# A two-layer row kernel on one core: row sums over sixteen rows, one ring of buffers for x and layer 0's outputs, later accumulating loads, and a PSUM ring turned by one tile

## The chip, the cores and the metric

The kernel runs on one core of a Trainium2 chip. The metric is the device time of one execution in microseconds. The engines are named as the profile names them: PE is TensorE (PEld its weight loads), DVE is VectorE, ACT is ScalarE, POOL is GpSimd, and SP is SyncE, which here only issues DMAs. A letter q after an engine (SPq) is its queue.

## What is computed

The input x has 384 x 384 positions of 128 channels, all in float32. Two layers follow one another. Layer 0 is a triangle update: a layer norm, two gated projections, a product over k for each channel, a second layer norm, an output projection and a gate, with x added. Layer 1 is a gated row mix: each row's output is scaled by the sum of `right` over that whole row, and a layer norm ends it.

```python
# layer 0
z = _layernorm(x, norm_g, norm_b)
left = (z @ Wl + bl) * jax.nn.sigmoid(z @ Wlg + blg)
right = (z @ Wr + br) * jax.nn.sigmoid(z @ Wrg + brg)
core = jnp.einsum('bikh,bjkh->bijh', left, right)
zo = _layernorm(core, onorm_g, onorm_b) @ Wout + bout
g = jax.nn.sigmoid(x @ Wg + bg)
x = x + g * zo
# layer 1, pair = x
left = pair @ W_left + b_left
right = pair @ W_right + b_right
gate = jax.nn.sigmoid(pair @ W_gate + b_gate)
left = left + (pair @ W_eq + b_eq)
right_sum = jnp.sum(right, axis=2, keepdims=True)
out = left * right_sum
out = out * gate
out = out @ W_out + b_out
return _layer_norm(out + pair, ln_scale, ln_bias)
```

## The kernel before

The program runs in three stages, one after the other, and every instruction is kept in the order in which the code writes it, on its engine's queue. What sets the order is therefore the code itself; what sets the time is which wait ends last.

**Stage 1 (to 1131 us)** goes over x in 144 chunks of eight rows by 128 positions. It makes row statistics (DVE), shifts x by them (POOL, L268), transposes (PE, L277), copies the result to SBUF (ACT, L279), and multiplies it with the four joined projection matrices (PE, L313) into a PSUM tile `pr` that holds two rows in two banks. ACT makes the sigmoid (L320) and DVE the gated product `lr` (L322), which empties the tile. `back` (L304) takes one `pr` tile for two rows, 576 in all, from a ring of three (`pps`, six banks); two single banks belong to `tps`. Ahead of the loop, one tile of the same ring, `p1`, serves the matmuls of `busy`, which only keep PE running while the first data arrive, and those of `fold`, which fold the norm's parameters into the weights. The stage stores its products `lr_d`, the shifted and transposed x `xt_d`, and the shifts `nd_d`.

**Stage 2 (1133 to 1876 us)** goes over the 128 hidden channels: 18 PE instructions for each (L477) into a PSUM tile `pc` of three banks, two such tiles in turn. POOL copies the right operand (L452 to L459), ACT and DVE copy the result out and sum it for the second norm.

**Stage 3 (1876 us to the end)** works in turns t, about one for each of the 384 rows. One turn does, for different rows:

- `front(f)`: PE's gate projection `pg` (L598) and ACT's sigmoid `gT`, for row f - 4. The transposed row `xT` comes, for the first 16 rows, from PE transposes (L609) and a copy into a work buffer; for later rows it is loaded as the sum of two DMAs into one tile of the ring `xp`: a plain broadcast load of `nd_d` (`load_x`, L548, SP's queue), and on top of it an accumulating load of `xt_d` (`add_x`, L556, POOL's queue).
- `scale_core(t)`: the core row times the norm's root, `cs` (POOL, L634). Its two operands are loaded by `load_core` (L566, L570) through SP's queue, into rings of three.
- `last` of the rows that were in layer 1 three turns before: DVE L718, which frees their PSUM tile `py`, then POOL L724.
- `right_sums(i0, i1)`: once all rows of a group are known, one small product `pq` of their column sums with W_right (L620), and its bias (DVE, L622), giving `rsum`.
- `layer0(t - 2)`: PE `pr` (L643), then two DVE operations (L644, L646); the second writes `x1T` and adds up its column sums into `tot`.
- `out_matrix`: ACT scales W_out by a row's `rsum` (L654).
- `gated_left(t - 3)`: PE `pg2` and `pl` (L660, L661; the profile calls both gate tiles pg), ACT `g2`, DVE `u` (L665).
- `layer1` and `stats1` for the rows that `at[t]` lists: PE L672 and L673 into `py` (a ring of four banks, `ps2`), DVE statistics (L687, L689), and for each second row POOL's root chain (L691 to L696), of which L692 is the power. `norm1` (ACT, L707) follows two turns later.

All other PSUM tiles of a turn (pg, pq, pr, pg2, pl) come from one ring of four banks, `ps`. At every fourth turn from t = 19 to 91 a list of `pieces` computes the rest of the second norm's root, on ACT, POOL and DVE, beside the turns.

A row can enter `layer1` only when its group's `rsum` is known, at the earliest three turns after the group's last row has come up. The table `turn` (L580 to L588) sets this: rows go one a turn, a group's first row not before `i1 + 3`, and near the end a row now and then shares the turn of the row before it, so that the lag shrinks. Before, groups have eight rows up to row 336, then four, and two in the last eight: 56 groups. The lag of layer 1 is 11 turns up to row 336 and 7 in the end; four turns (347, 354, 361, 368) hold two rows of layer 1 on the way, and 383 and 386 in the tail.

Buffers in SBUF: `fp` holds `xT` and `gT`, 13 each; `lp` holds `x1T` and `u`, 11 each; `wp` four each of `cs`, `g2` and `wo`. In stage 3 the pools lie in the space that stages 1 and 2 have left.

Of the kernel before, what the change touches and what calls it, by code (L numbers as in the profile page):

```python
# [8 lines left out]
F32 = mybir.dt.float32  # L9
# [5 lines left out]
P = 128  # L15
# [4 lines left out]
def triangle_then_gated_row_kernel(ctx: ExitStack, tc: tile.TileContext, a: dict, out: bass.AP):  # L20
# [13 lines left out]
    x = a["x"].rearrange("b i j c -> (b i) j c")  # L34
    y = out.rearrange("b i j c -> (b i) j c")
    N, _, C = x.shape
    H = a["L0_conv_Wl"].shape[1]
# [7 lines left out]
    A = 9  # L45
# [35 lines left out]
    with ExitStack() as ctx2:  # L81
# [17 lines left out]
        with tc.tile_pool(name="p1w", bufs=6, side="right") as wp, \  # L99
# [46 lines left out]
            warm = const([P, 1], "warm")  # L146
            seq(nc.scalar.activation(warm, mhalf[:, 0:1], AF.Sigmoid))
            wz = const([P, 4 * H], "wz")
            p1 = pps.tile([P, 2, 4 * H], F32, tag="pr", name="p1")[:, 0]
            pgb = tps.tile([P, 4, P], F32, tag="pt", name="pgb")[:, 0, 0:2]  # L150
            g0 = const([P, 1], "g0")

            def busy(n):

                for _ in range(n):
                    seq(nc.tensor.matmul(
                        p1, lhsT=avg, rhs=avg.unsqueeze(1).to_broadcast([P, 4, P]), start=True, stop=True
                    ))

            def fold():  # L160
# [357 lines left out]
    with ExitStack() as ctx3:  # L518
        def pool(name, bufs, **kw):
            return ctx3.enter_context(tc.tile_pool(name=name, bufs=bufs, reuse_waits="tile", **kw))  # L520

        xp, fp, inp, op = pool("p3x", 6), pool("p3f", A + 4), pool("p3in", 3), pool("p3out", 3)
        wp, sp = pool("p3w", 4), pool("p3s", 4)
        lp = pool("p3l", 11)
        ps2, ps = pool("p3ps2", 4, space=PSUM), pool("p3ps", 4, space=PSUM)

        def bank(name):
# [1 line left out]

        def work(name, pool=wp):  # L530
            return pool.tile([P, N], F32, tag=name, name=name)

        cols = [slice(b * P, (b + 1) * P) for b in range(NB)]
        lnsb = lns.unsqueeze(1).to_broadcast([P, NB, C])
# [41 lines left out]

        firsts = list(range(0, N - 48, 8)) + list(range(N - 48, N - 8, 4)) + list(range(N - 8, N, 2))
        group, sums, turn = {}, {}, []  # L580
        for i0, i1 in zip(firsts, firsts[1:] + [N]):
            sums[i1 + 2] = i0, i1
            for i in range(i0, i1):
                group[i] = i0, i - i0
                t = turn[-1] + 1 if i else 0
                turn.append(max(i1 + 3, t - (i0 >= N - 48 and i % 8 == 1 and t > i + 7 or i in (N - 7, N - 3))))
        assert turn[N - 8:] == [N - 1, N - 1, N, N + 1, N + 2, N + 2, N + 3, N + 4]
        at = {t: [i for i in range(N) if turn[i] == t] for t in range(N + 5)}  # L588

# [3 lines left out]
        def front(f):  # L593

            r = rows.get(f - L)
            if r:
                pg = bank("pg")
                seq(nc.tensor.matmul(pg[:, :N], lhsT=wg0, rhs=r["xT"], start=True, stop=True))  # L598
                gT = r["gT"] = work("gT", fp)
                seq(nc.scalar.activation(gT, pg[:, :N], AF.Sigmoid, bias=bg0))  # L600
            if f < N:
                i0, n = f // RG * RG, f % RG
                if f >= TR:
                    xT = xts[i0][:, n]
                else:
                    xT = work("xT", fp)
                    pxt = ps2.tile([P, 512], F32, tag="py", name="pxt") if f < A else bank("pxt")
                    for s in cols:
                        seq(nc.tensor.transpose(pxt[:, s], xin[i0][:, n, s], ident))  # L609
                    if 4 <= f < A:  # L610
                        seq(nc.vector.tensor_copy(xT, pxt[:, :N]))
                    else:
                        seq(nc.scalar.copy(xT, pxt[:, :N]))
                rows[f] = {"xT": xT}

        def right_sums(i0, i1):

            q = quad[i0]
            pq = bank("pq")
            seq(nc.tensor.matmul(pq[:, :i1 - i0], lhsT=wright, rhs=q["tot"][:, :i1 - i0], start=True, stop=True))  # L620
            q["rsum"] = sp.tile([P, 8], F32, tag="rsum", name="rsum")
            seq(nc.vector.tensor_scalar(q["rsum"][:, :i1 - i0], pq[:, :i1 - i0], bright, None, ALU.add))  # L622

        def scale_core(i):
# [11 lines left out]
        def layer0(i):  # L636

            r = rows[i]
            m, n = group[i]
            if n == 0:  # L640
                quad[m] = {"tot": sp.tile([P, 8], F32, tag="tot", name="tot")}
            pr = bank("pr")
            seq(nc.tensor.matmul(pr[:, :N], lhsT=wc, rhs=r["cs"], start=True, stop=True))  # L643
            seq(nc.vector.scalar_tensor_tensor(pr[:, :N], pr[:, :N], bz, r["gT"], ALU.add, ALU.mult))  # L644
            x1T = r["x1T"] = work("x1T", lp)
            seq(nc.vector.scalar_tensor_tensor(  # L646
                x1T, pr[:, :N], bout1, r["xT"], ALU.add, ALU.add, accum_out=quad[m]["tot"][:, n:n + 1]
            ))
# [7 lines left out]
        def gated_left(i):  # L656

            r = rows[i]
            pg2, pl = bank("pg2"), bank("pl")
            seq(nc.tensor.matmul(pg2[:, :N], lhsT=wgate, rhs=r["x1T"], start=True, stop=True))  # L660
            seq(nc.tensor.matmul(pl[:, :N], lhsT=wleft, rhs=r["x1T"], start=True, stop=True))  # L661
            g2 = work("g2")
            seq(nc.scalar.activation(g2, pg2[:, :N], AF.Sigmoid, bias=bgate))  # L663
            u = r["u"] = work("u", lp)
            seq(nc.vector.scalar_tensor_tensor(u, pl[:, :N], bleft, g2, ALU.add, ALU.mult))  # L665

        def layer1(i, py):
# [80 lines left out]
        for t in range(N + 3):  # L748

            while f < min(N + L, t + max(L, A - t // 3)):  # L750
                front(f)
                f += 1
            if t % RG == 0:
                load_core(t + 2 * RG)
            if t >= 2 and fetched <= f + 16:
                load_x(fetched)
                fetched += RG
            if t >= 7 and (t % 4 == 1 or t < 12) and added <= f + 8:
                add_x(added)
                added += RG  # L760
            if t < N:
                scale_core(t)
            if t >= 16 and t % 4 == 3 and pieces:
                step, b, s = pieces.pop(0)
                step(b, s)
                if step is root:
                    step, b, s = pieces.pop(0)
                    step(b, s)
                if step is newton and s == cols[-1]:
                    store_rstd(b)  # L770
            done = at.get(t - 3, [])
            for i in done:
                last(i)
            if t in sums:
                right_sums(*sums[t])
            if 2 <= t < N + 2:
                layer0(t - 2)
            for i in at[t + 1]:
                out_matrix(i)
            if t >= 3:  # L780
                gated_left(t - 3)
            for i in at[t]:
                layer1(i, ps2.tile([P, 512], F32, tag="py", name="py"))
                stats1(i)
            for i in at.get(t - 2, []):
                norm1(i)
            store()
# [53 lines left out]
```

## Time and profile before

| | |
|---|---|
| median of 3 runs | 3296.77 us (3295.2 to 3296.97) |
| the profiled execution | 3295.14 us, span 3293.4 us |
| granted clock, mean | 0.998 |
| L313 PE MATMUL, stage 1 | 1040.1 us busy, x2304 |
| L477 PE MATMUL, stage 2 | 743.3 us busy, x2304 |
| L620 PE MATMUL (pq) | 15.9 us busy, x112 |
| L692 POOL (root chain) | 257.9 us busy, x192, mean 1343 ns |
| L556 POOL DMA issue | 85.8 us busy, x92, mean 932 ns; landing 6.7, 9.5, 15.3 us (least, median, most) |
| POOL and DVE from 2400 to 2800 us | 348.70 and 351.02 us busy of 400 |
| DMA engines from 2400 to 2800 us | 0.97 of their time, 273 GB/s |

Busy time is summed over an engine's instructions; a float32 product shows as two matmul records, a transpose as one. The records of consecutive matmuls overlap, so it is their starts that are to be compared. The number behind an arrow is the idle time of the engine ahead of an instruction, and the name is that of the instruction that ended the wait.

### The profile page before, as it was taken

To read this page: it belongs to the slowest core of one execution; us is meant where nothing else is said; L and a number is where in the kernel's file an instruction comes from. 1 tells how busy PE (TensorE), PEld (TensorE's weight loads), DVE (VectorE), ACT (ScalarE), POOL (GpSimd) and SP (SyncE) were. 2 spreads that over 40 slices of the span, in tenths; PEclk is the share of its full clock that TensorE was granted. 3 is DMA by queue.
4 is the path that set the end of the run, shared out by engine and by line. 5 is a ranking of instruction groups with operands and counts; after the bars stand their busy time and mean duration, and the time that the engine had idled before them with its cause. 6 is when DMAs were issued, how large, how long until landed. Compare 5 with 4: busy or idle time off the path is not lost.

```text
span 3293.4 us, 48397 instructions
## 1 busy us (share of the span) xinstructions
PE 3269.7 (99%) x12496; PEld 1991.3 (60%) x12496; DVE 2500.1 (76%) x8040; ACT 1940.3 (59%) x4055; POOL 2287.2 (69%) x3300
## 2 busy tenths in 40 slices
PE   9999999999999999999999999999999999999998
PEld 4544444444444566666666666767777777777776
DVE  7777777777777655555555588888888888888888
ACT  4555555555555433334333467777777777777776
POOL 6555555555555566656566578898888888888887
PEclk9999999999999999999999999999999999999999
DMA  6998998998999499999999999999999999999993
GB/s 164 273 279 259 277 280 258 275 281 260 276 281 263 148 284 279 284 282 285 281 286 282 286 295 265 277 273 274 276 270 274 279 271 268 278 278 269 275 260 109
DMA packets 922056, 873.72 MB, mean 265 GB/s; under 512 B 24834, under 2 KB 836868, under 8 KB 921780
## 3 DMA queue, kind: packets, MB, share of 16 engines
q1 hardware_dynamic: 906532, 796.03, 78.3%
q0 software_dynamic: 13440, 72.56, 12.9%
q8 instruction: 103, 1.69, 0.2%
q10 hardware_dynamic: 1808, 2.03, 0.2%
q14 instruction: 173, 1.42, 0.1%
HBM read 508.63 MB, written 361.89 MB: 264 GB/s over the span
## 4 chain that ended last, share of the span: by engine, by line
PE 94%; POOL 3%; DVE 1%; ACT 1%; DMA 1%; issue 1%; POOLq 0%; DVEq 0%; ACTq 0%
PE pr L313 30%; PE pc L477 23%; PE py L672 7%; PE pr L643 7%; PE pg L598 7%; PE pl L661 7%; PE pg L660 7%; PE pt L277 4%; PE py L673 3%; POOL cs L634 1%; POOL rs L692 1%; POOL yt L724 1%; DMA xt<-nd_d 1%; ACT py L707 0%; DVE st L687 0%
## 5 line engine op out<-in xcount | busy, mean ns | idle before, releaser
L313 PE MATMUL pr<-wz,zt 128*128 128x512 f32 x2304 | 1040.1, 593 | 0.7 <-ACT zt L279 0.7
L320 ACT ACTIVATE sg<-pr,rs 128x256 f32<-128x256 f32 x1152 | 483.8, 471 | 497.9 <-PE pr L313 361.3
L477 PE MATMUL pc<-rr,lrh 128*128 128x384 f32 x2304 | 743.3, 486 | 2.0 <-DVE lr L322 2.0
L322 DVE SCALAR_TENSOR_TENSOR lr<-pr,rs,sg 128x256 f32<-128x256 f32 x1152 | 504.8, 480 | 267.5 <-ACT sg L320 218.8
L313 PEld LDWEIGHTS pr<-wz,zt 128*128 128x128 f32 x2304 | 414.2, 190 | 411.0 <-issue 345.9
L477 PEld LDWEIGHTS pc<-rr,lrh 128*128 128x128 f32 x2304 | 452.0, 196 | 293.6 <-issue 2.8
L707 ACT ACTIVATE py<-py,nm,rs 128x128 f32<-128x128 f32 x1149 | 494.5, 431 | 198.1 <-POOL rs L696 115.0
L672 PEld LDWEIGHTS py<-wo,u 128*128 128x128 f32 x2304 | 377.1, 191 | 100.6 <-DVE yt L718 0.6
L634 POOL TENSOR_TENSOR cs<-ct,rt 128x384 f32<-128x384 f32 x380 | 428.5, 1131 | 4.9 <-DMA rt<-rstd_d 4.9
L488 DVE TENSOR_TENSOR csum<-csum,ct 128x1152 f32<-128x1152 f32 x127 | 176.8, 1392 | 333.9 <-ACT ct L486 333.9
L724 POOL TENSOR_TENSOR yt<-yt,lnb 128x384 f32<-128x384 f32 x380 | 425.6, 1121 | 3.4 <-DVE yt L718 3.2
L486 ACT COPY ct<-pc 128x1152 f32<-128x1152 f32 x127 | 142.2, 1120 | 446.9 <-PE pc L477 446.9
L672 PE MATMUL py<-wo,u 128*128 128x128 f32 x2304 | 402.7, 275 | 0.3 <-ACT wo L654 0.3
L258 POOL TENSOR_SCALAR sd<-mv 128x8 f32<-128x8 f32 (+1 forms) x145 | 28.7, 198 | 427.4 <-DVE mv L245 427.3
L268 POOL TENSOR_TENSOR z<-xt,nd 128x512 f32<-128x512 f32 x288 | 300.4, 1043 | 34.6 <-POOL z L268 29.4
L687 DVE BATCH_NORM_STATS2 st<-py 128x6 f32<-128x128 f32 x1152 | 266.1, 287 | 76.0 <-PE py L673 74.5
L643 PE MATMUL pr<-cs,wc 128*128 128x384 f32 x768 | 315.2, 492 | 1.3 <-POOL cs L634 1.3
L673 PE MATMUL py<-ident,x1T 128*128 128x128 f32 x1152 | 314.0, 273 | 0.0
L661 PE MATMUL pl<-x1T,mat_L_conv_W_left 128*128 128x384 f32 x768 | 311.5, 487 | 1.4 <-ACT gT L600 1.4
L660 PE MATMUL pg<-x1T,mat_L_conv_W_gate 128*128 128x384 f32 x768 | 310.8, 486 | 1.1 <-ACT g L663 0.9
L598 PE MATMUL pg<-xt,mat_L_conv_Wg 128*128 128x384 f32 x736 | 298.4, 487 | 0.0
L458 POOL COPY rr<-lrh 128x768 f32<-128x768 f32 x128 | 176.3, 1378 | 159.5 <-DMA lrh<-lr_d 159.4
(129 smaller groups left out, 4932.5 us busy)
## 6 DMA issues: line engine op xcount, KB each, us to landing
lr_d<-lr SPq DMA_DIRECT2D x128, 1024.0 KB, 7.1
lrh<-lr_d SPq DMA_DIRECT2D x128, 768.0 KB, 7.7
xt_d<-zt SPq DMA_DIRECT2D x288, 256.0 KB, 5.5
xt<-in_x_dram SPq DMA_DIRECT2D x143, 512.0 KB, 6.3
ct<-core_d SPq DMA_DIRECT2D x95, 768.0 KB, 6.1
rt<-rstd_d SPq DMA_DIRECT2D x95, 768.0 KB, 7.6
out_dram<-yt SPq DMA_DIRECT2D x94, 768.0 KB, 8.9
core_d<-ct SPq DMA_DIRECT2D x125, 576.0 KB, 8.8
```

The costliest lines, as they stand in the source:

```text
L313: seq(nc.tensor.matmul(pr[:, r, :], lhsT=zts[n, q][:, 2 * half + r, :], rhs=wz, start=True, stop=True))
L320: seq(nc.scalar.activation(sg[r], pr[:, r, 2 * H:], AF.Sigmoid, scale=rs[r]))
L322: seq(nc.vector.scalar_tensor_tensor(t[:, :, c * XR + r0 + r, :], pr[:, r, :2 * H].rearrange("k (h s) -> k h s", s=2), rs[r], sg[r].rearra ...
L477: seq(nc.tensor.matmul(banks[ib], lhsT=t[:, kb, ib * P:(ib + 1) * P, 0], rhs=rr[:, kb], start=(kb == 0), stop=(kb == NB - 1),))
L598: seq(nc.tensor.matmul(pg[:, :N], lhsT=wg0, rhs=r["xT"], start=True, stop=True))
L634: seq(nc.gpsimd.tensor_tensor(cs, ct[:, i % RG], rt[:, i % RG], ALU.mult))
L643: seq(nc.tensor.matmul(pr[:, :N], lhsT=wc, rhs=r["cs"], start=True, stop=True))
L660: seq(nc.tensor.matmul(pg2[:, :N], lhsT=wgate, rhs=r["x1T"], start=True, stop=True))
L661: seq(nc.tensor.matmul(pl[:, :N], lhsT=wleft, rhs=r["x1T"], start=True, stop=True))
L672: seq(nc.tensor.matmul(py[:, s], lhsT=r["u"][:, s], rhs=r["wo"], start=True, stop=False))
L707: seq(nc.scalar.activation(py[:, s], py[:, s], AF.Identity, bias=bias, scale=scale))
L724: seq(engine.tensor_tensor(yt, yt, lnbb, ALU.add))
```

## The change

It has four parts.

1. Stage 1 takes two tiles from the ring of `pr` ahead of the loop, not one: `p0` for `busy`, `p1` for `fold`. Each later `pr` tile lies one slot further round the ring.
2. In stage 3, `xT` of the first 16 rows and `x1T` share one ring of 20 buffers (tag x in `lp`), `u` gets a pool of its own with 18, and `gT` has 9. The pools are opened in another order, and so lie at other addresses.
3. The groups of the row sums have 8, 8, 8, 12, 12, then sixteen times 16, six times 8, six times 4 and four times 2 rows: 37 groups. `tot` and `rsum` become 16 wide. By the table `turn`, no row enters layer 1 in turns 35 to 38 and 63 to 66, the lag of layer 1 is 19 turns for rows 48 to 305, and twelve turns (every fourth from 324 to 368) hold two rows; 383 and 386 stay as they are.
4. The accumulating loads begin in turn 9 and go out in every fourth turn. Rows 16, 20, 24 and 28 are issued in turns 9, 13, 17 and 21; before, in turns 7, 8, 10 and 17. In the steady part a load is issued 7 turns ahead of its first use and not 11.

```diff
-            p1 = pps.tile([P, 2, 4 * H], F32, tag="pr", name="p1")[:, 0]
+            p0, p1 = (pps.tile([P, 2, 4 * H], F32, tag="pr", name=n)[:, 0] for n in ("p0", "p1"))
...
-                        p1, lhsT=avg, rhs=avg.unsqueeze(1).to_broadcast([P, 4, P]), start=True, stop=True
+                        p0, lhsT=avg, rhs=avg.unsqueeze(1).to_broadcast([P, 4, P]), start=True, stop=True
...
-        xp, fp, inp, op = pool("p3x", 6), pool("p3f", A + 4), pool("p3in", 3), pool("p3out", 3)
-        wp, sp = pool("p3w", 4), pool("p3s", 4)
-        lp = pool("p3l", 11)
+
+        xp, lp, fp, inp = pool("p3x", 6), pool("p3l", 20), pool("p3f", A), pool("p3in", 3)
+        wp, sp, op, up = pool("p3w", 4), pool("p3s", 4), pool("p3out", 3), pool("p3u", 18)
...
+        def work_x(name):
+
+            return lp.tile([P, N], F32, tag="x", name=name)
...
-        firsts = list(range(0, N - 48, 8)) + list(range(N - 48, N - 8, 4)) + list(range(N - 8, N, 2))
+        sizes = [8] * 3 + [12] * 2 + [16] * ((N - 128) // 16) + [8] * 6 + [4] * 6 + [2] * 4
+        assert sum(sizes) == N
         group, sums, turn = {}, {}, []
-        for i0, i1 in zip(firsts, firsts[1:] + [N]):
+        i1 = 0
+        for size in sizes:
+            i0, i1 = i1, i1 + size
             sums[i1 + 2] = i0, i1
             for i in range(i0, i1):
                 group[i] = i0, i - i0
                 t = turn[-1] + 1 if i else 0
-                turn.append(max(i1 + 3, t - (i0 >= N - 48 and i % 8 == 1 and t > i + 7 or i in (N - 7, N - 3))))
+                turn.append(max(i1 + 3, t - (i >= N - 80 and i % 5 == 1 and t > i + 7 or i in (N - 7, N - 3))))
...
-                    xT = work("xT", fp)
+                    xT = work_x("xT")
...
-            q["rsum"] = sp.tile([P, 8], F32, tag="rsum", name="rsum")
+            q["rsum"] = sp.tile([P, 16], F32, tag="rsum", name="rsum")
...
-                quad[m] = {"tot": sp.tile([P, 8], F32, tag="tot", name="tot")}
+                quad[m] = {"tot": sp.tile([P, 16], F32, tag="tot", name="tot")}
...
-            x1T = r["x1T"] = work("x1T", lp)
+            x1T = r["x1T"] = work_x("x1T")
...
-            u = r["u"] = work("u", lp)
+            u = r["u"] = work("u", up)
...
-            if t >= 7 and (t % 4 == 1 or t < 12) and added <= f + 8:
+            if t >= 9 and t % 4 == 1:
                 add_x(added)
                 added += RG
```

## The prediction

> **What bounds the kernel now.** I read three views in this order: the page (busy times, slices, chain), the timeline of single stretches, and the table of waits.
>
> ```profile
> PE 3269.7 (99%) x12496; PEld 1991.3 (60%) x12496; DVE 2500.1 (76%) x8040; ACT 1940.3 (59%) x4055; POOL 2287.2 (69%) x3300
> ...
> POOL 6555555555555566656566578898888888888887
> ...
> PE 94%; POOL 3%; DVE 1%; ACT 1%; DMA 1%; issue 1%; POOLq 0%; DVEq 0%; ACTq 0%
> ```
>
> PE is busy 99% of the span and is 94% of the chain. So the change can gain only by removing PE work or one of PE's few idle stretches, about 24 us in all (3293.4 - 3269.7), much of it at the very start and end. Everything it adds to other engines is free unless PE comes to wait for it. In the last stage (from 1876 us) POOL is the next busiest.
>
> PE's timeline in the last stage prices a group's row sum:
>
> ```profile
> 2513.23 0.81 PE L598 MATMUL pg<-xt,mat_L_conv_Wg 128*128 128x384 f32 x2
> 2513.88 0.81 PE L643 MATMUL pr<-cs,wc 128*128 128x384 f32 x2
> 2514.52 0.81 PE L660 MATMUL pg<-x1T,mat_L_conv_W_gate 128*128 128x384 f32 x2
> ...
> 2516.81 0.81 PE L598 MATMUL pg<-xt,mat_L_conv_Wg 128*128 128x384 f32 x2
> 2517.46 0.28 PE L620 MATMUL pq<-tot,mat_L_conv_W_right 128*128 128x8 f32 x2
> 2517.60 0.89 PE L643 MATMUL pr<-cs,wc 128*128 128x384 f32 x2
> 2518.32 0.81 PE L660 MATMUL pg<-x1T,mat_L_conv_W_gate 128*128 128x384 f32 x2
> ```
>
> A turn repeats every 3.58 us (2513.23 to 2516.81). From pg (L598) to pg2 (L660) it takes 1.29 us without the row sum and 1.51 us with it: **0.22 us a group**. Near the end, at 3250.76 us, a group of two rows gives the same 1.51, so columns hardly enter.
>
> The boundary of stages 1 and 2, PE then DVE:
>
> ```profile
> 1127.41 3.60 PE L313 MATMUL pr<-wz,zt 128*128 128x512 f32 x8
> 1133.05 1.21 PE L477 MATMUL pc<-rr,lrh 128*128 128x384 f32 x3 [2.04 <-DVE lr L322]
> ```
> ```profile
> 1130.21 0.88 DVE L322 SCALAR_TENSOR_TENSOR lr<-pr,rs,sg 128x256 f32<-128x256 f32 x2 [0.95 <-ACT sg L320]
> 1131.92 0.88 DVE L322 SCALAR_TENSOR_TENSOR lr<-pr,rs,sg 128x256 f32<-128x256 f32 x2 [0.84 <-ACT sg L320]
> ```
>
> The first stage-2 matmul starts 0.25 us after DVE has emptied the last pr tile (1132.80). The tile before that was empty at 1131.09.
>
> The start of stage 3, POOL then PE:
>
> ```profile
> 1900.01 0.94 POOL L556 DMA_DIRECT2D xt<-xt_d  x1 [3.91 <-DMA xt<-nd_d]
> 1900.65 1.32 POOL L634 TENSOR_TENSOR cs<-ct,rt 128x384 f32<-128x384 f32 x1
> 1901.78 1.06 POOL L556 DMA_DIRECT2D xt<-xt_d  x1
> 1902.39 2.42 POOL L634 TENSOR_TENSOR cs<-ct,rt 128x384 f32<-128x384 f32 x2
> 1913.33 0.88 POOL L556 DMA_DIRECT2D xt<-xt_d  x1 [8.52 <-DMA xt<-nd_d]
> 1913.94 3.19 POOL L634 TENSOR_TENSOR cs<-ct,rt 128x384 f32<-128x384 f32 x3
> ```
> ```profile
> 1915.29 0.91 PE L643 MATMUL pr<-cs,wc 128*128 128x384 f32 x2 [1.35 <-POOL cs L634]
> ```
>
> The third accumulating load, in turn 10, sits in POOL's queue before that turn's cs and waits 8.52 us for its plain load; PE ends by waiting for that cs.
>
> **What the skill says.** *TensorE: Matmul & The Clock Gate*, Part 2, "Step-by-step", says the next weights are loaded while the current matmul runs. The trace agrees for full tiles (a 0.19 us load under 0.81 us of matmul); eight columns are too short a cover, which fits the flat 0.22 us. The same page, Part 1, "Architectural detail", calls ACT, DVE and GpSimd strict FIFOs: the cs held behind the load above is that. *PSUM — Partial Sum Buffer*, "PSUM bank collisions", says to guard PSUM by bank: the 2.04 us wait is such a guard, on a buffer and not on data. *DMA: Bandwidth & Descriptors*, "SWDGE vs HWDGE", says only GpSimd can issue accumulating DMAs; here each issue holds POOL for 0.93 us.
>
> **The change, part by part.** Figures are against the profiled execution, 3295.14 us (span 3293.4).
>
> *Groups.* 56 groups become 37. Nineteen row sums go, 19 x 0.22 = **-4.2 us** on PE. The 16 remaining wide ones stream eight columns more; at 0.645/384 us a column that is 0.013 us each, 0.2 us in all if none hides, 0 if all does: I take 0. DVE loses 19 x 0.216 us, off the path.
>
> *Bank waits.* With a pq the turn takes five tiles of the ring of four, so pl needs the bank of the same turn's pg, which ACT must read first. The trace shows PE idle there at 2025, 2055, 2113, 2143 and 2201 us (0.17 to 0.35 us); with the restart these turns are 0.53, 0.52, 0.61, 0.44 and 0.62 us longer than other pq turns, 2.7 us together. All lie where the pieces of the root run (turns 19 to 91), which make ACT's norms late. That stretch had row sums in turns 26, 34, 42, ... 90; it now has them in 26, 38, 50, 66 and 82, two of them in light turns. I keep two stalls of 0.45: **-1.8 us**, between 0 and -2.7. The stall at 2032 us (table loads for the root) stays.
>
> *PSUM ring.* The ring has three tiles. One more tile at its head moves the last of the 576 pr tiles off the slot that stage 2 opens in; that slot's last user is now the one before, free at 1131.09, so pc can start at 1131.34, but PE is only done at 1131.01. **-1.7 us**, or 0 if stage 2's three banks touch both slots. Next late would be the copies into rr for the third k-block: they follow the last lr and end at 1133.3, needed 12 matmuls x 0.32 = 3.9 us after the start, 1135.2. POOL's copies for the second channel end at 1135.2, needed at 1137.1. Covered. The busy matmuls only change their target.
>
> *Accumulating loads.* Same 92 issues, now rows 16, 20, 24 in turns 9, 13, 17, not 7, 8, 10. On POOL, cs 7 and 8 move ahead of the first, cs 9 to 12 ahead of the second; core loads waiting in SP's queue for those cs (L566 at 1902.00) go out earlier. The load for row 24, landed at 1913.3, is asked for only around 1934. PE's hole is 1915.29 - 1913.78 = 1.5 us plus 0.1 of restart: **-1.6 us**; 0 if rt for row 12, issued at 1891.78 into saturated DMA, is as late. Later each load is issued 7 turns before its row is used, 25 us (21 through the light turns), not 11; landing takes 6.7 to 15.3 us. Covered.
>
> *Rings and schedule.* xT and x1T share 20 buffers, u gets 18, gT 9. Layer 1 follows its row by up to 19 turns, so x1T's buffer is free 3 turns before it is rewritten and u's 2: 0 us, and cover lost only if layer 1 slipped two turns (7 us). The new addresses keep early tiles out of stage 2's latest buffers; PE's waits there (0.56 us on PSUM, 0.23 on x1T data) aren't about addresses: 0. Turns 35 to 38 and 63 to 66 have no layer 1 (light, four matmul pairs, 2.58 us); in exchange twelve turns, every fourth from 324 to 368, have two (before: four, every seventh). PE's total is the same. But POOL: four turns take it 13.4 us (2500.19 to 2513.57), a fifth row adds yt 0.96 and half a root chain 1.08, so 15.4 us against PE's 4 x 3.58 + 1.00 + 0.22 = 15.5. Before, seven turns with eight rows were 25.5 against 26.3, and PE lost 0.15 us (its row period at 3180 was 4.72, not 4.57). The cost of a double is thus between 0 and POOL's whole extra 2.04 us; I take 0.07 each, **+0.8 us**, since POOL still just fits.
>
> Sum: -4.2 - 1.8 - 1.7 - 1.6 + 0.8 = **-8.5 us**. The profiled execution would be 3286.6; the median of runs, 1.6 us higher before (3296.77), gives 3288.3: I say 3288.
>
> **Rivals.** *B, part of it only:* PE gets just the row sums; ring and start are replaced by a next wait, and the bank stalls move to other turns. 3296.77 - 4.2 = 3292.6. For: the pieces of the root still fall beside row sums, and DMA is at 1.01 of its share from 1890 to 1920. Against: the next releases computed above have 1.9 us or more of slack. *C, slower:* POOL sets the pace in the twelve double turns. If its 2.04 us comes wholly on top each time, 24.5 - 9.3 = +15: 3312. It undoes the gain from 0.8 us a double on. For: 99% load, and py's four banks leave no spare turn after a double. Against: the four doubles before nearly ran free.
>
> **How the numbers follow.** Forecast 0.64, B 0.24, C 0.12. About 0.2% (6.6 us) is what tells from no change: the forecast lies beyond it, B within. C passes it in 0.09 and stays within in 0.03: faster 0.64, same 0.27, slower 0.09. Low end: all gains at their full size, no cost, 10.2, and 2 of scatter: 3284.5. High end: B with some cost in the doubles: 3294.
>
> **What would show it.** Right: 74 pq matmuls (before 112); pc starting within 0.4 us of the last pr; no PE wait on cs around 1914; fewer waits of pl on gT; double turns at 4.57 us. Wrong: double turns of 5 us and more, with py waiting for yt (L718) and L707 for rs; pc still waiting for lr; PE waiting for cs or xt in turns 12 to 16.

## The result, and the profile after

| | before | after |
|---|---|---|
| median of 17 runs each | 3296.17 us (3294.28 to 3298.72) | 3289.34 us (3288.54 to 3290.4) |
| after / before, 95% interval | | 0.998 (0.9972 to 0.9987) |
| the profiled execution | 3295.14 us, span 3293.4 us | 3289.21 us, span 3287.4 us |
| first pg2 (L660, now L667) of row 14, of row 376 | 1933.29, 3248.47 us | 1929.64, 3242.29 us |

The change is worth 6.8 us by the medians, 4.3 to 9.2 us by the interval, and 5.9 us between the two profiled executions (6.0 by their spans). In the whole text that follows "after" is the changed kernel; its line numbers in stage 3 are 4 higher than those of before in the loads and 7 higher from `front` on.

Two lines of the page of after: busy times, and the chain by engine.

```profile
PE 3265.1 (99%) x12458; PEld 1986.6 (60%) x12458; DVE 2481.1 (75%) x8021; ACT 1933.4 (59%) x4055; POOL 2281.7 (69%) x3300
...
PE 91%; POOL 6%; ACT 1%; issue 1%; DMA 1%; DVE 1%; POOLq 0%; ACTq 0%
```

PE lost 4.6 us of work (3269.7 to 3265.1) and still bounds the kernel. But POOL's share of the chain has doubled, from 3% to 6%. That is a first hint of where a part of the gain stayed.

The boundary of stages 1 and 2 in after, PE and then DVE:

```profile
1127.17 3.60 PE L313 MATMUL pr<-wz,zt 128*128 128x512 f32 x8
1131.09 9.28 PE L477 MATMUL pc<-rr,lrh 128*128 128x384 f32 x28 [0.32 <-DVE lr L322]
```
```profile
1129.96 0.88 DVE L322 SCALAR_TENSOR_TENSOR lr<-pr,rs,sg 128x256 f32<-128x256 f32 x2 [0.95 <-ACT sg L320]
1131.68 0.88 DVE L322 SCALAR_TENSOR_TENSOR lr<-pr,rs,sg 128x256 f32<-128x256 f32 x2 [0.84 <-ACT sg L320]
```

Stage 2's first product starts 0.25 us after the last but one `pr` tile is empty (1129.96 + 0.88 = 1130.84) and while DVE still has the last one to empty. PE's idle time there is 0.32 us where it was 2.04.

The start of stage 3 in after, POOL:

```profile
1897.99 0.93 POOL L560 DMA_DIRECT2D xt<-xt_d  x1 [0.75 <-DMA xt<-nd_d]
1899.16 1.00 POOL L641 TENSOR_TENSOR cs<-ct,rt 128x384 f32<-128x384 f32 x1 [0.24 <-PE pr L650]
1902.07 1.00 POOL L641 TENSOR_TENSOR cs<-ct,rt 128x384 f32<-128x384 f32 x1 [1.91 <-PE pr L650]
```

POOL waits 0.75 us for a plain load, not 3.91 and 8.52, and what its cs waits for is PE, which has yet to read an older one of the four cs buffers: POOL is now ahead. PE comes from row 8 to row 14 (pg2 to pg2) in 20.17 us instead of 21.79.

A turn of after with a row sum of sixteen rows, number 98, which loses time. First PE, then ACT.

```profile
2215.96 0.81 PE L605 MATMUL pg<-xt,mat_L_conv_Wg 128*128 128x384 f32 x2
2216.61 0.29 PE L627 MATMUL pq<-tot,mat_L_conv_W_right 128*128 128x16 f32 x2
2216.75 0.89 PE L650 MATMUL pr<-cs,wc 128*128 128x384 f32 x2
2217.48 0.81 PE L667 MATMUL pg<-x1T,mat_L_conv_W_gate 128*128 128x384 f32 x2
2218.90 0.91 PE L668 MATMUL pl<-x1T,mat_L_conv_W_left 128*128 128x384 f32 x2 [0.61 <-ACT gT L607]
```
```profile
2216.99 1.36 ACT L714 ACTIVATE py<-py,nm,rs 128x128 f32<-128x128 f32 x3 [1.67 <-POOL rs L703]
2218.28 0.57 ACT L607 ACTIVATE gT<-pg,col_L_conv_bg 128x384 f32<-128x384 f32 x1
```

From pg to pg2 it is 1.52 us, as with eight rows (1.51): the sixteen columns cost what eight did. The last PE line is the bank wait of the prediction. ACT's queue shows its reason: the norm of an older row (L714) stood waiting 1.67 us for POOL's root chain, gT stood behind it, and pl needs the bank that gT reads.

The table of waits of after (who waited for whom: us in all, times, longest):

```profile
PEld pl L668 <- ACT gT L607: 4.6, 7, 1.2
...
POOL xt L560 <- DMA xt<-nd_d: 0.7, 1, 0.7
...
PE pg L605 <- ACT gT L607: 1.3, 2, 0.8
```

Before, pl's wait for gT stood at 8.0 us in 13 cases, and POOL's wait for the plain load at 12.4. The third line is new: pg itself, the first product of a turn, waits for gT. It belongs to the short turns, and there the prediction went wrong.

The short turns 35 to 38 in after: POOL, ACT and PE around 1996 us.

```profile
1995.19 1.36 POOL L699 TENSOR_TENSOR rs<-rs,mhalf 128x6 f32<-128x6 f32 x1
...
1996.91 0.20 POOL L703 TENSOR_SCALAR rs<-rs 128x6 f32<-128x6 f32 x1
```
```profile
1995.35 0.58 ACT L670 ACTIVATE g<-pg,col_L_conv_b_gate 128x384 f32<-128x384 f32 x1 [0.31 <-PE pg L667]
1997.15 1.36 ACT L714 ACTIVATE py<-py,nm,rs 128x128 f32<-128x128 f32 x3 [1.22 <-POOL rs L703]
1998.43 0.57 ACT L607 ACTIVATE gT<-pg,col_L_conv_bg 128x384 f32<-128x384 f32 x1
```
```profile
1995.79 0.81 PE L605 MATMUL pg<-xt,mat_L_conv_Wg 128*128 128x384 f32 x2
...
1997.73 0.81 PE L668 MATMUL pl<-x1T,mat_L_conv_W_left 128*128 128x384 f32 x2
1999.06 0.91 PE L605 MATMUL pg<-xt,mat_L_conv_Wg 128*128 128x384 f32 x2 [0.52 <-ACT gT L607]
```

A turn without layer 1 takes PE 2.58 us instead of 3.58. ACT and POOL still have the norms and roots of the rows that entered two and three turns earlier, at their old pace. So ACT's norm waits 1.22 us for POOL (done at 1997.11), gT stands behind it in ACT's queue and starts only at 1998.43, and the next turn's pg finds no free bank until 1998.43 + 0.57.

To put a number on each such place, I took the starts of pg2 for all rows and subtracted what a turn is due: 2.582 us, 0.994 for each row of layer 1, 0.22 for a row sum. A turn is counted up to its own pg2; what pl loses in turn 98 therefore stands under 99. Between the rows 14 and 376 the surplus is 5.47 us before and 7.12 us after, and it divides as follows.

| place | before | after | difference |
|---|---|---|---|
| turns with a row sum, pl on gT | 3.77 (0.15 to 0.62 in seven turns from 35 to 99, and little ones) | 2.33 (0.78 at 51, 0.87 at 99, and little ones) | -1.44 |
| the two blocks of short turns | | 2.49 (0.79 at 37, 0.35 at 38, 1.03 at 65, 0.35 at 66) | +2.49 |
| about the turns with two rows | 0.0 | 0.58 (0.23 at 344, 0.24 at 352) | +0.58 |
| table loads for the root, turns 44 and 45 | 1.16 | 1.16 | 0 |
| all turns, 1 to 2 ns each | 0.54 | 0.56 | 0 |

With -4.2 for the row sums, -1.7 at stage 2's start, -1.6 at stage 3's, about -0.2 in stage 1 and +0.2 behind row 376 this is -5.9 us, where the spans differ by 6.0.

These surpluses are read from one execution each. How far they repeat is seen in `e1_ring` below, which is the same code as before in these turns: 4.92 us in all where before has 5.47. A difference of some tenths of a microsecond between two kernels is therefore not told from chance.

### The profile page after: what moved, and what is told of

Its sections match the earlier page's. It is cut to its first block, busy times and chain, and to the rows that moved or that the text cites. A ratio compares the mean times of both kernels' runs of the same rounds, so it can differ in the third digit from the quotient of the medians.

```text
span 3287.4 us, 48321 instructions
## 1 busy us (share of the span) xinstructions
PE 3265.1 (99%) x12458; PEld 1986.6 (60%) x12458; DVE 2481.1 (75%) x8021; ACT 1933.4 (59%) x4055; POOL 2281.7 (69%) x3300
## 3 DMA queue, kind: packets, MB, share of 16 engines
q8 instruction: 102, 1.67, 0.2%
## 4 chain that ended last, share of the span: by engine, by line
PE 91%; POOL 6%; ACT 1%; issue 1%; DMA 1%; DVE 1%; POOLq 0%; ACTq 0%
PE pr L313 30%; PE pc L477 22%; PE py L679 6%; PE pl L668 6%; PE pr L650 6%; PE pg L667 6%; PE pg L605 6%; PE pt L277 4%; PE py L680 3%; POOL rs L699 2%; POOL yt L731 1%; POOL cs L641 1%; ACT py L714 1%; DMA core_d<-ct 0%; POOL rs L698 0%
## 5 line engine op out<-in xcount | busy, mean ns | idle before, releaser
L714 ACT ACTIVATE py<-py,nm,rs 128x128 f32<-128x128 f32 x1149 | 493.1, 430 | 196.8 <-POOL rs L703 117.8
L667 PE MATMUL pg<-x1T,mat_L_conv_W_gate 128*128 128x384 f32 x768 | 310.8, 486 | 1.1 <-ACT g L670 0.9
L458 POOL COPY rr<-lrh 128x768 f32<-128x768 f32 x128 | 187.4, 1464 | 158.4 <-DMA lrh<-lr_d 158.3
```

What stands on the lines that cost most here:

```text
L714: seq(nc.scalar.activation(py[:, s], py[:, s], AF.Identity, bias=bias, scale=scale))
```

## The experiments

Theory 1 is: the four parts act each by itself, as predicted, and the missing time is lost at the short turns, where PE outruns ACT and POOL. The rivals: the losses are those of the pieces of the root, which would cost the same with any table of turns; and the parts depend on each other.

**One part of the change alone.** The first two start from before, the third from after.

`e1_ring`: the first two hunks of the diff (`p0` and `p1`) alone, in the kernel before.

> The kernel before with one more tile at the head of stage 1's PSUM ring, nothing else. Theory: this alone moves the wait of stage 2's first matmul from the last pr tile to the one before it. PE's pause there falls from 2.0 us to 0.3, the rest of the trace stays, the time falls by 1.7 us (3296.2 to 3294.5). Rival (the gain at this boundary came with other parts of the change, for instance another place in SBUF): the pause stays at 2.0 us and the time at 3296.

`e2_adds`: the accumulating loads alone, in the kernel before.

```diff
-            if t >= 7 and (t % 4 == 1 or t < 12) and added <= f + 8:
+            if t >= 9 and t % 4 == 1:
```

> The kernel before with the accumulating loads from turn 9 on in every fourth turn, nothing else. Theory: PE's pause of 1.35 us on cs near 1915 us goes, POOL's two waits for the plain load (3.9 and 8.5 us) shrink to under 1 us in all, and nothing else moves: 1.6 us less (3294.6). Rival (the hole closed because the buffers of xT and x1T changed): the pause on cs stays near 1.3 us, time 3296. The stalls of pl on gT in turns 35 to 91 should stay at 3.0 us.

`e3_groups`: after with these two edits put back, so that groups, table of turns and buffers remain.

> The changed kernel with the ring of stage 1 and the accumulating loads put back as before: groups, turn table and buffers alone. Theory, by the sums of the changed kernel's trace: 19 row sums less, -4.2 us; stalls in the turns without layer 1 and of pl on gT, +0.9 against before; double turns, +0.7; so -2.6 us (3293.6), with PE's pause of 1.35 us on cs at the start of stage 3 and its 2.0 us before stage 2 both there. Rival (the shared ring does part of the work at the start): the pause on cs is gone, -4.2 us (3292.0).

Measured: 3292.99, 3293.88 and 3294.57 us, medians of 12 runs each, beside 3295.87 for before in the same runs; ratios 0.9994 (0.9986 to 1.0003), 0.9995 (0.9987 to 1.0003) and 0.9999 (0.9990 to 1.0007). No single interval leaves 1, and the medians alone (2.9, 2.0 and 1.3 us less) settle nothing, so it is the traces that decide. PE's timeline of `e1_ring`, at the two places:

```profile
1130.89 2.50 PE L477 MATMUL pc<-rr,lrh 128*128 128x384 f32 x7 [0.32 <-DVE lr L322]
...
1913.33 0.91 PE L643 MATMUL pr<-cs,wc 128*128 128x384 f32 x2 [1.55 <-POOL cs L634]
```

PE's timeline of `e2_adds`:

```profile
1132.20 2.18 PE L477 MATMUL pc<-rr,lrh 128*128 128x384 f32 x6 [2.04 <-DVE lr L322]
...
1912.93 0.81 PE L643 MATMUL pr<-cs,wc 128*128 128x384 f32 x2
```

And of `e3_groups`:

```profile
1132.90 1.74 PE L477 MATMUL pc<-rr,lrh 128*128 128x384 f32 x3 [2.04 <-DVE lr L322]
...
1917.16 0.91 PE L650 MATMUL pr<-cs,wc 128*128 128x384 f32 x2 [1.73 <-POOL cs L641]
```

Each pause goes with its own edit and with no other: the ring takes 1.72 us at stage 2 and leaves the 1.5 us at turn 14; the loads take that (row 8 to row 14: 20.18 us) and leave the 2.04. Without both, the groups shorten the way from row 14 to row 376 from 1315.18 to 1312.51 us, by 2.67: the short turns lose 2.7 us there (1.03, 0.35, 1.01, 0.35). So these parts act independently of each other as far as the pauses show, and the loss of the short turns is in the groups' part. Two expectations of `e2_adds` were missed: POOL's wait for a plain load was to fall below 1 us and is 1.3, and the row-sum turns from 35 to 91 were to go on losing 3.0 us and lost 2.2.

In `e3_groups` stage 2 also took 1.7 us more than before (first pc to first pxt, 744.82 against 743.12 us), though PE waited for nothing more. The view by windows has the reason (window, PE's busy time with its instructions, granted clock, DMA share and GB/s):

```profile
1130.00:1134.00 4.00, 1.96 (x6) 0.93 0.51 136
1134.00:1138.00 4.00, 4.00 (x9) 0.64 0.71 257
1138.00:1142.00 4.00, 4.00 (x14) 1.00 0.06 12
```

From 1133.45 to 1136.86 us, just behind the pause of 2.04 us, the granted clock was 0.50; 3.41 us at half the clock lose 1.7. Before has the same pause and a clock of 1.00 there in its profiled execution, so this comes in some executions and not in others, and nothing ties it to the groups.

**Spreading the short turns.** `e4_spread`: the eight turns without layer 1 stand apart (19, 24, 29, 34 and 43, 48, 53, 58), with the groups as they are.

```diff
-                t = turn[-1] + 1 if i else 0
+                t = turn[-1] + 1 + (i in (8, 12, 16, 20, 28, 32, 36, 40)) if i else 0
```

> The changed kernel with its eight turns without layer 1 spread: not turns 35 to 38 and 63 to 66 in a row but one before each of rows 8, 12, 16, 20, 28, 32, 36 and 40. PE's work, groups and row sums are the same. Theory 1 (four short turns in a row let PE run ahead of ACT, whose norms wait for POOL's root chain, and the next pg waits for gT): single short turns leave ACT time to catch up, the stalls of 0.79, 0.35, 1.03 and 0.35 us in turns 36 to 38 and 64 to 66 go, 2.0 to 2.5 us less than the changed kernel (3287.0). Rival (the pieces of the root, which stand in turns 35 and 63, make those turns late): stalls of the same size stay in the short turns that have a piece or follow one, time within 0.5 us of the changed kernel (3289.3).

Measured: 3289.44 us (21 runs; ratio to before 0.998, 0.9974 to 0.9987), the same as after. That is the time that the rival named, but the trace is not the rival's: the losses at 36 to 38 and 64 to 66 are gone, as theory 1 says. But turn 44, where ACT loads the tables for the root, now loses 2.04 us instead of 1.04, and turn 45 loses 1.78 instead of 0.11. PE's timeline in turn 44, and two windows (columns as above):

```profile
2024.26 1.46 PE L667 MATMUL pg<-x1T,mat_L_conv_W_gate 128*128 128x384 f32 x2 [1.88 <-ACT g L670]
```
```profile
2020.00:2024.00 4.00, 2.38 (x8) 1.00 1.02 265
...
2026.00:2028.00 2.00, 2.00 (x8) 0.52 1.04 398
```

Two things meet here. The short turn 43 brings PE one microsecond earlier to a place where ACT is late anyway, and the microsecond is given back: the pause grows to 1.88 us. And behind it the clock is at 0.50, from 2024.49 to 2027.90 us, which is the 1.67 us at 45; pg2 itself takes 1.46 us and not 0.81. In `e7_both` below, with the same pause of 1.88 us, the clock stayed at 1.00 in the profiled execution and turn 45 lost 0.11. The 21 times of `e4_spread` agree: six lie from 3287.17 to 3288.18 us, fifteen, the profiled one among them, from 3289.07 to 3289.71. The mean granted clock of an execution says the same: it is 0.997 in nine of the fifteen and in none of the six. If the six are those without the drop, which only a trace of one could show, spreading alone is worth about 1.5 us, and the drop behind its pause mostly costs it again.

**The pieces of the root.** `e5_pieces_late`: the pieces start in turn 71, not 16.

```diff
-            if t >= 16 and t % 4 == 3 and pieces:
+            if t >= 71 and t % 4 == 3 and pieces:
```

> The changed kernel with the pieces of the second norm's root begun in turn 71, not 19, so that none stands in or near the turns without layer 1. Theory 1 (four short turns in a row outrun ACT): the stalls in turns 36 to 38 and 64 to 66 stay at 2.0 to 2.5 us together, and the time stays within 0.5 us of the changed kernel (3289.3), the pieces' own stalls (1.15 us for the table loads, those of pl on gT) only moving to later turns. Rival (the pieces make those turns late): the stalls go from turns 36 to 38 and 64 to 66, and 2 us less (3287.2) unless the pieces cost the same elsewhere.

Measured: 3291.39 us (21 runs; 0.9986, 0.9979 to 0.9993). Three lines of PE's timeline, the first two at the short turns and the third among the pieces' new turns:

```profile
1998.78 0.91 PE L605 MATMUL pg<-xt,mat_L_conv_Wg 128*128 128x384 f32 x2 [0.28 <-ACT gT L607]
...
2096.32 0.91 PE L605 MATMUL pg<-xt,mat_L_conv_Wg 128*128 128x384 f32 x2 [0.30 <-ACT gT L607]
...
2209.60 0.91 PE L667 MATMUL pg<-x1T,mat_L_conv_W_gate 128*128 128x384 f32 x2 [1.27 <-ACT g L670]
```

With no piece anywhere near, the short turns still lose 1.8 us of their 2.5 (0.54, 0.36, 0.56, 0.36). So the pieces are about 0.7 us of it, and four short turns in a row cost 0.9 us by themselves. The pieces bring their own losses along to the later place (1.43 us at 96, 1.30 at 147, 0.75 at 83), which is why the time is worse. Neither expectation held as it stood: the losses at the short turns are between the theory's 2.0 to 2.5 us and the rival's nothing, and the time rose by 2 us.

**The row sum behind pl.** `e6_pq_behind`: in a turn with a row sum, pq comes last, so that pl is the fourth tile of the ring and no longer the fifth. The scaled W_out that needs the sum moves back with it.

```diff
-            if t in sums:
-                right_sums(*sums[t])
             if 2 <= t < N + 2:
                 layer0(t - 2)
+            if t >= 3 and t in sums:
+                gated_left(t - 3)
+            if t in sums:
+                right_sums(*sums[t])
             for i in at[t + 1]:
                 out_matrix(i)
-            if t >= 3:
+            if t >= 3 and t not in sums:
                 gated_left(t - 3)
```

> The changed kernel with the row sum pq and its turn's scaled W_out moved behind pg2 and pl of the same turn. Theory (with pq ahead of pr, five tiles of a ring of four make pl wait for the same turn's gT on ACT): the stalls of pl on gT in turns 51 and 99 (0.78 and 0.87 us) and the small ones of 0.2 to 0.3 us in turns 259 and 375 go, 1.5 to 2.0 us less (3287.6); the stalls in turns 36 to 38 and 64 to 66 stay, less the two of 0.35 where pq waits for ACT's g. Rival (ACT is simply late there, and PE waits at another tile of the ring instead, or W_out comes too late for layer 1): stalls of 0.5 us or more on another wait in the same turns, time within 0.5 us of 3289.3, or up to 0.4 us more for each of 31 groups if wo is late.

Measured: 3287.97 us (8 runs; 0.9974, 0.9964 to 0.9984), 1.4 us below after. PE's timeline in turn 50, and pq in turn 98:

```profile
2047.35 0.81 PE L668 MATMUL pl<-x1T,mat_L_conv_W_left 128*128 128x384 f32 x2
2048.27 0.39 PE L627 MATMUL pq<-tot,mat_L_conv_W_right 128*128 128x12 f32 x2
...
2218.68 0.40 PE L627 MATMUL pq<-tot,mat_L_conv_W_right 128*128 128x16 f32 x2 [0.20 <-ACT gT L607]
```

pl starts right behind pg2; the fifth tile, pq, inherits the wait, later and shorter: turns 51 and 99 lose 0.39 and 0.46 where they lost 0.78 and 0.87. Turn 99 is the clearer of the two: it loses 0.87 to 0.89 in `e3_groups`, `e4_spread` and `e8_spread2` as well, while turn 51 loses only 0.49 in `e3_groups`, with the same turns. So this wait is one on a bank, as the prediction said, and not on data, and moving the tile that makes it five is worth about half of it. The short turns keep their loss (0.96 at 37, 1.35 at 65).

**Both, and other places for the short turns.** `e7_both` is `e4_spread` with `e6_pq_behind`; `e8_spread2` has its short turns in 21, 24, 29, 34 and 49, 54, 57, 62, away from the table loads; `e9_spread2_pq` is that with pq behind pl. The edit shown is that of `e8_spread2`.

```diff
-                t = turn[-1] + 1 if i else 0
+                t = turn[-1] + 1 + (i in (10, 12, 16, 20, 34, 38, 40, 44)) if i else 0
```

> The changed kernel with both: the turns without layer 1 spread, and pq behind pl. If both theories hold and the two are independent, 3.5 to 4.5 us less than the changed kernel (3285.2), PE's stalls from turn 17 to 380 down from 7.1 us to under 3, of which 1.15 for the table loads. If the stalls only move, 3288 to 3289.

> The changed kernel with its eight turns without layer 1 at 21, 24, 29, 34, 49, 54, 57 and 62: single, and not in turn 43, where the root's two table loads hold ACT, nor in any other turn with a piece. Theory 1 (four short turns in a row outrun ACT; in the first spread version the gain was lost because a short turn lay on the table loads): no stall in turns 36 to 38 and 64 to 66, about 1.0 us left in turn 44, stalls from row 14 to row 376 down from 7.1 to 4.5 us, 2.0 to 2.5 us less than the changed kernel (3287.0). Rival (ACT and POOL are at their limit in that stretch, so what one turn gains another loses): stalls of the same sum in other turns before 100, time within 0.5 us of 3289.3.

> The same placement of the turns without layer 1, and pq with its turn's scaled W_out moved behind pg2 and pl. If both causes add up: stalls from row 14 to row 376 about 3.2 us (1.1 for the table loads, 0.5 in turn 99, 0.9 in the double turns), 3.5 to 4.0 us less than the changed kernel (3285.5). If they overlap: 3286.8, as the first alone.

| kernel | median (runs) | ratio to before | surplus from row 14 to 376 | of it |
|---|---|---|---|---|
| after | 3289.34 (17) | 0.998 (0.9972 to 0.9987) | 7.12 | see above |
| `e4_spread` | 3289.44 (21) | 0.998 (0.9974 to 0.9987) | 7.45 | 44: 2.04, 45: 1.78 (the clock), 60: 0.39, 99: 0.88 |
| `e7_both` | 3286.76 (7) | 0.9971 (0.9960 to 0.9982) | 5.15 | 44: 2.04, 60: 0.43, 99: 0.47 |
| `e8_spread2` | 3288.27 (10) | 0.9977 (0.9968 to 0.9986) | 6.27 | 26: 0.66, 44: 1.04, 50: 0.76, 51: 1.01, 99: 0.88 |
| `e9_spread2_pq` | 3286.41 (6) | 0.9972 (0.9960 to 0.9983) | 4.76 | 44: 1.04, 51: 1.37, 99: 0.46 |

None of the three came up to its expectation (3285.2, 3287.0 and 3285.5 us): the losses that were to go came back in part in other turns.

Spread away from the table loads and with pq behind pl, the first four short turns cost 0.3 us (0.13 at 26, 0.16 at 36). The second four cost 1.4 to 1.8 us wherever I put them up to here: in `e9_spread2_pq`, which has the lowest median here (2.9 us below after; the intervals of the ratios overlap), turn 51 alone loses 1.37 us, two turns behind a short one. PE's timeline of `e9_spread2_pq`, turn 44 and turn 50:

```profile
2024.01 0.91 PE L667 MATMUL pg<-x1T,mat_L_conv_W_gate 128*128 128x384 f32 x2 [0.88 <-ACT g L670]
...
2047.14 0.39 PE L627 MATMUL pq<-tot,mat_L_conv_W_right 128*128 128x12 f32 x2 [1.03 <-ACT gT L607]
```

**Why the second four cost.** Two further places for them. `e11_spread3_pq` has them in 53, 56, 61 and 64, behind the row sum of turn 50. `e12_late_set` has them in 93, 96, 103 and 108, behind the last piece (turn 91), which needs groups of twelve up to row 95. Both have pq behind pl; the edit shown is that of `e12_late_set`.

```diff
-        sizes = [8] * 3 + [12] * 2 + [16] * ((N - 128) // 16) + [8] * 6 + [4] * 6 + [2] * 4
+        sizes = [8] * 3 + [12] * 6 + [16] * ((N - 176) // 16) + [8] * 6 + [4] * 6 + [2] * 4
...
-                t = turn[-1] + 1 if i else 0
+                t = turn[-1] + 1 + (i in (10, 12, 16, 20, 78, 80, 86, 90)) if i else 0
```

> The changed kernel with pq behind pl and the turns without layer 1 at 21, 24, 29, 34, 53, 56, 61 and 64: none just ahead of the row sum of turn 50. Theory (a short turn uses up PE's slack against ACT, and a wait that needs the same slack one turn later, a row sum or the table loads, then stalls): the stall of 1.37 us that turn 51 had with a short turn at 49 falls under 0.5, stalls from row 14 to row 376 fall from 4.8 to about 3.8 us, 1 us less than with 49 (3285.4). Rival (a short turn costs its stall wherever it stands): the stall moves to turns 54 to 66 and the time stays at 3286.4.

> The spread version with the row sum behind pl, but rows 48 to 95 stay in groups of 12 (38 groups, one row sum more), so that the second four short turns come after the pieces have ended: turns 93, 96, 103 and 108. Theory 'the second four short turns cost because they fall beside the pieces of the root, whose work keeps ACT and POOL without slack': the stall of 1.37 us in turn 51 shrinks to under 0.5, the turns from 93 to 112 lose under 0.4 us together beyond their due times, and the time is about 1 us below the version with turns 49, 54, 57 and 62 (3286.4 us), near 3285.4 (one row sum of 0.22 us added). Rival 'four more short turns cost 1.4 to 1.9 us wherever they stand, since ACT and POOL need time to catch up with a PE that is four row's work ahead': PE waits for gT or g appear from turn 93 on, 1.4 us or more together, and the time is 3286.6 or above.

Measured: `e11_spread3_pq` 3286.85 us (9 runs; 0.9974, 0.9964 to 0.9984). Turn 51 falls from 1.37 to 0.36 us, as expected, but two others take it over, 0.85 at 58 and 0.65 at 66, both waits of pg for gT, as its rival said.

`e12_late_set`: 3286.78 us (9 runs; 0.9974, 0.9964 to 0.9983). Turn 51 loses 0.35, the turns from 93 to 112 lose 1.05, and of this 0.92 falls at 95, behind the first of the four; the short turns 96, 103 and 108 cost 0.13, 0 and 0. New losses of 0.14 and 0.46 appear at 73 and 75, beside a row sum that the twelves put into turn 74. Neither expectation was met: the loss is less than 1.4 and more than 0.4 us, while the total is what the rival said. PE and POOL around turn 95:

```profile
2206.61 0.91 PE L605 MATMUL pg<-xt,mat_L_conv_Wg 128*128 128x384 f32 x2 [0.49 <-ACT gT L607]
```
```profile
2198.15 0.45 POOL L419 TENSOR_TENSOR r<-r,ve 128x128 f32<-128x128 f32 x1
...
2199.07 0.46 POOL L421 TENSOR_TENSOR r<-r,m 128x128 f32<-128x128 f32 x1
...
2204.47 0.20 POOL L703 TENSOR_SCALAR rs<-rs 128x6 f32<-128x6 f32 x1
```

POOL was still behind from the last piece (1.2 us of it) when the first short turn came, and its root chain ended at 2204.67. The other three cost nearly nothing. How full POOL is beside the pieces is seen in windows of 40 us of after (the columns are the window, then each engine's busy time with its instructions, clock, DMA share and GB/s):

```profile
1940.00:1980.00 40.00, 40.00 (x192) 28.11 (x191) 35.30 (x128) 30.43 (x73) 38.02 (x53) 1.00 0.95 268
...
2220.00:2260.00 40.00, 40.00 (x196) 28.34 (x195) 35.63 (x124) 28.82 (x67) 34.83 (x49) 1.00 0.98 272
```

38.0 us of 40 beside the pieces, 34.8 behind them. This fits: an engine with 2 us of free time in 40 can't follow a PE that gets ahead by one microsecond in each of four turns, and one with 5 us can, when they stand apart. That POOL's backlog sets the second four's cost in each of these tables was not shown, and the surpluses of the last three (4.76, 5.58 and 5.06 us) are too close for one execution each to rank them. The cause of the loss of 0.87 us at 99, of which pq behind pl took half, stays open too.

**The price of a row sum, by doubling it.** `e10_pq_twice`: after, with the product of every row sum issued twice into the same bank.

```diff
-            seq(nc.tensor.matmul(pq[:, :i1 - i0], lhsT=wright, rhs=q["tot"][:, :i1 - i0], start=True, stop=True))
+            for _ in range(2):
+                seq(nc.tensor.matmul(
+                    pq[:, :i1 - i0], lhsT=wright, rhs=q["tot"][:, :i1 - i0], start=True, stop=True
+                ))
```

> The changed kernel with each of its 37 row sums computed twice into the same bank; buffers, waits and everything else are unchanged. Theory (a row sum holds PE for 0.22 us, nearly all of it weights that so few columns can't cover): 37 x 0.22 = 8.1 us more (3297.5). Rival (most of the 0.22 us is the switch of weights between two full tiles, paid once): 2 to 5 us more (3292 to 3294), and then the term of the row sums was right by its difference only.

Measured: 3295.80 us (13 runs; ratio to before 1.0002, 0.9994 to 1.001), 6.5 us above after. PE's timeline of a row-sum turn far from all losses (pg2 stands in L670 here):

```profile
2506.02 0.81 PE L605 MATMUL pg<-xt,mat_L_conv_Wg 128*128 128x384 f32 x2
2506.67 0.51 PE L628 MATMUL pq<-tot,mat_L_conv_W_right 128*128 128x16 f32 x4
...
2507.76 0.81 PE L670 MATMUL pg<-x1T,mat_L_conv_W_gate 128*128 128x384 f32 x2
```

From pg to pg2 it is 1.74 us, 0.22 more than with one: 37 times 0.22 is 8.1 us. That the time rises by 6.5 only is the waits again: with 0.44 us counted as due for a row sum, the surplus of these turns falls from 2.3 to 1.4 us and that about the turns with two rows from 0.6 to 0.1. The second product fills time in which PE would wait. The time lies between the two expectations, 1.7 us below the theory's 3297.5 and 1.8 above the rival's 3294. It is the 0.22 us between pg and pg2 that speaks for the full price.

## Why the prediction held, and which step of it failed

The forecast was a gain of 8.5 us and a time of 3288; 6.8 us and 3289.34 were measured. In the profiled executions, on which its sums rest, it was further off: 3286.6 forecast, 3289.21 measured. The forecast then added 1.6 us, by which the median of before lay above its profile; for after that distance is 0.1. Nothing in the prediction said that it would shrink, so that the medians came within 1.3 us is in good part luck. Its steps in turn:

- *Groups*, -4.2: right. 74 pq matmul records, and the pg to pg2 distance with and without doubling confirm 0.22 us each, whatever the columns.
- *Bank waits*, -1.8: the cause was right, as `e6_pq_behind` shows; that the sum is near, -1.4, is partly chance. Beside the pieces, where the prediction looked for two stalls of 0.45, one of 0.78 us stayed. The other, 0.87 us at turn 99 where before has 0.16, lies behind the last piece, where it expected none.
- *PSUM ring*, -1.7: right, 1.72, alone and with the rest. The two covers named there held: no wait of PE on rr came in its place. Not foreseen was that the clock can fall just behind the pause that it removes (`e3_groups`, 1.7 us).
- *Accumulating loads*, -1.6: right (21.79 to 20.17 us), alone too (21.79 to 20.18).
- *Rings and schedule*, +0.8 for the doubles: near in the sum, 0.6, but by luck. Its ground was a misreading: the 4.72 us near 3180 are the way from pr to pr (3180.32 to 3185.04), with the row sum of the next turn in it (3184.90); from pg to pg that turn takes 4.58 (3179.67 to 3184.25), and PE lost nothing. Nor does each turn cost 0.07: two places, 344 and 352, hold 0.23 and 0.24, and no other over 0.04. In after, near 3138 us, a turn with two rows goes from pg2 to pg2 in 4.58 us (3138.74 to 3143.32), so POOL doesn't set the pace, and rival C is out.
- *Rings and schedule*, the light turns at nothing: **this is the step that failed**. "PE's total is the same" is true of PE's work and says nothing of its waits. The runs showed 2.5 us there instead: PE gets 1 us ahead in each light turn, ACT and POOL keep working for older rows, and with four such turns in a row ACT's norm, waiting for POOL's root chain, holds back gT and so the bank for pg. In `e4_spread` this loss goes when the turns stand apart; `e5_pieces_late` shows that 1.8 us of it are there with no pieces near.

With the light turns at +2.5 the forecast's own sum is -6.0, and the profiled executions differ by 5.9 us. The medians differ by 0.9 more. Drops of the clock behind the pauses that only before has would do that, and the times point there: those of before lie over 4.4 us, those of after over 1.9; and of the 49 executions of before that stand beside the single-part runs, the 11 with a mean clock of 0.997 take 1.4 us more on average than the 35 with 0.998. No trace shows one of these slower executions of before, so this stays open. Rival B (row sums only, 3292.6) is refuted for the ring and the loads by the traces of the two single-part runs, where no next wait takes the place of the pause. Its other half came true in part: bank stalls did move to other turns, as that at 99 did.

## What to carry to other kernels

A bound engine's idle slots are only half of what a schedule must keep in view: a turn in which this engine has less to do is a turn in which it outruns the others, so look up how much free time the next busiest engines have there, and whether their work of earlier rows shrinks at the same moment. Where a turn must be shortened, set such turns apart and away from stretches with extra work; and put the tile that overfills a ring of banks at the end of the turn, where its wait is shorter. To find a few microseconds, subtract what each turn is due from the distance of its starts: the list of surpluses says where, when the run's time can't.

## What the runs showed that I had not expected

- The same small product, repeated with the same weights right behind itself, costs its full 0.22 us again (`e10_pq_twice`). PE's weight loads in that turn show four loads for the four records, none left out:

```profile
2506.35 0.74 PEld L628 LDWEIGHTS pq<-tot,mat_L_conv_W_right 128*128 128x128 f32 x4
```

- Doubling an operation on the engine that bounds the kernel did not cost its full price: 6.5 of 8.1 us. Between rows 14 and 376 the waits shrank by 1.4 us. Read backwards, taking away work just before a wait should give less than its price; that was not run.
- A pause of PE of about 2 us may cost nearly as much again. The profiles hold five pauses of 2.04 or 1.88 us between 1130 and 2025 us. Behind two of them (`e3_groups`, `e4_spread`) the granted clock was 0.50 for 3.41 us, and 1.7 us were lost; behind the same pauses in before, `e2_adds` and `e7_both` it stayed at 1.00. The shorter pauses of the second and third stage, up to 1.73 us, had none behind them. That the pause brings the drop is not shown by an experiment, and three profiles (before, after, `e6_pq_behind`) also have one such stretch between 11 and 16 us, at the kernel's start. So what else sets it is open. The Trainium skill, *TensorE: Matmul & The Clock Gate*, Part 1, "What's actually happening", describes a clock that falls to half after an idle window of about 3.4 us, and windows that run on regardless of the program. Half a clock for one such window would lose 1.7 us by that page, an estimate that the 1.67 and 1.70 us meet, and the free windows would explain why it comes and goes. But here the drop came behind pauses of 1.9 and 2.0 us, shorter than that window, and the measurement decides.
